# Moving the operand ring and the weights to multiples of 128 bytes, and splitting the first tile's gated layer by token blocks

## The chip, the core and the metric

The kernel runs on one NeuronCore of a Trainium2 chip. The metric is the device time of one execution in microseconds (us); lower is better. A NeuronCore has a matrix engine (PE, which also loads its stationary operands; those loads are shown as PEld), a vector engine (DVE), a scalar engine (ACT), a general engine (POOL) and a sync engine (SP). Each takes its own instructions in order, and semaphores order them against each other. Matmul operands lie in SBUF, an on-chip memory of 128 partitions, and results go to PSUM, which has 8 banks of 128 x 512 floats.

## The reference

The inputs are `x` (8 batches x 256 tokens x 256), `ctx` (8 x 120 x 256) and the ternary weights (-1, 0, 1) of a feed-forward net with a scale for each output feature.

```python
x = x + xattn(layernorm(x), ctx)        # per batch: gelu(xn ctx^T) * (xn ctx^T), times ctx
h = silu(lin(z, w1) * s1) * (lin(z, w2) * s2)   # z = layernorm(x); 256 -> 1024
h = gelu(lin(h, h1) * sh1)                      # 1024 -> 1024, exact gelu
h = gelu(lin(h, h2) * sh2)                      # 1024 -> 1024
x = x + lin(h, w3) * sw3                        # 1024 -> 256
```

Everything is float32.

## The kernel before

**Tiles and stages.** The 2048 tokens are four tiles of 512 tokens; a tile is two batches, a batch two token blocks of 128. The program runs in three stages that overlap only at their seams.

1. *Attention and gated layer* (`Attention.run`, lines 208 to 294, and `gated`, lines 418 to 454). For each batch: layernorm statistics on DVE (L232, L236, L237), the root on POOL (L242), the normalised rows `xn` (L252 on DVE, or L249 on ACT), PE transposes (L264), scores (L269), a tanh form of gelu on ACT and DVE (L282 to L287), values (L274), the residual (L290), a second layernorm, transposes again, and `finish` (L399, L400), which writes the transposed rows as two float32r tiles: `hi` is the rounded value and `lo` the rest, so that two passes of the faster float32r matmul give float32 accuracy. Then the gated layer: for each of 8 feature groups `m`, 8 matmuls (two sides, `hi` and `lo`, two halves of the contraction), a Silu on ACT (L450) and a product on DVE (L452).
2. *The two hidden layers* (`hidden`, lines 491 to 551), done on pairs of tiles by a seven-product scheme (Strassen-Winograd). `operand` (line 473) rounds an operand into a slot `hi` and the rest into `lo` (L480 on ACT, L484 on DVE); `product` (L511) runs, for each of four output groups, 4 matmuls of 128 x 512 on `hi` and 4 on `lo`. The slots are a ring of three pairs of tiles, `hi0..2` and `lo0..2`, made in `open_later` (line 611) in a pool on the right side of SBUF. The very first product uses another pair, `op0`, which lies on the left side beside the weights `w0..w6`. The stage has 864 matmuls on the ring and 32 on `op0`.
3. *The output layer* (`output`, L562): 256 matmuls of 128 x 256 with the ring's tiles as the stationary operand and `w3` as the moving one; then two DVE instructions (L297, L298) and a store (L582) for each token block.

**Order.** All of it is recorded in a `Plan`: every entry has an engine, a cost in us, what it reads and writes and a `lag` until its result can be used. `issue` (line 140) ranks the entries by the longest path behind them, changes some ranks by random seeds listed in `PICKS`, runs a list scheduler with these costs, and emits the instructions in the order that comes out. The costs of a matmul are `PE = 0.1185` for 256 columns and `PE2 = 0.2265` for 512 (lines 162, 163). Loads have a landing time, their `lag`: line 203 gives 2.2 us for the pieces of batch 0, 3.5 for batch 1 and 4.0 for all others; line 206 has 2.5 and 4.0 for the context.

**Names that the change touches.** `NORM_ON_ACT = 2` (line 43): from batch 2 on, the normalised rows come from ACT, with an extra DVE instruction (L239) and POOL instruction (L244) for it. `HALVED = 2` (line 42): tiles 0 and 1 run the gated layer by batches, so that its matmuls have 256 columns; tiles 2 and 3 by the whole tile, 512 columns. `turn` (line 414) hands out PSUM banks 0 to 4 in rotation. `const` and `keep` are pools on the left of SBUF, filled upwards; `early` and `later` are on the right, filled so that their end is fixed.

Of the kernel before, what the change touches and what calls it, by code (L numbers as in the profile page):

```python
# [10 lines left out]
F32 = mybir.dt.float32  # L11
# [9 lines left out]
P = 128  # L21
NB = 8
S = 256
# [8 lines left out]
RING = 3  # L32

PICKS = (
    17, 35, 50, 83, 119, 135, 167, 184, 208, 217, 248, 283, 296, 346, 414, 434, 469, 491, 533,
    575, 610, 675, 710, 726, 818, 898, 1040, 1072, 1715, 1745, 1774, 1894, 1946, 2086, 2179,
    2192, 2221, 2298, 2311, 2410, 2929, 3422, 4202, 4298, 4888, 5025, 5171, 5227, 5233, 5618,
    5767, 5867, 6269, 9944, 11293, 46856, 46885, 47139, 49461,
)
FORCE_GENERAL = False  # L40

HALVED = 2
NORM_ON_ACT = 2

# [18 lines left out]
class Plan:  # L65
# [6 lines left out]
    def add(self, engine, weight, emit, r=(), w=(), lag=0.2, early=0.0, chain=None):  # L72
        i, deps = len(self.ops), {}
        for k in r:
            if k in self.writer:
                deps[self.writer[k]] = True
            self.readers.setdefault(k, []).append(i)
        for k in w:
            if k in self.writer:
                deps[self.writer[k]] = True  # L80
            for j in self.readers.pop(k, ()):
                if j != i:
                    deps[j] = True
            self.writer[k] = i
        if chain is not None:
            if chain in self.last:
                deps.setdefault(self.last[chain], False)
            self.last[chain] = i
        self.ops.append((engine, weight, emit, deps, lag, early))
# [72 lines left out]
PE = 0.1185  # L162
PE2 = 0.2265
# [3 lines left out]
def xattn_ffn_kernel(ctx: ExitStack, tc: tile.TileContext, x, ctx_b, wall, scal, s3, out):  # L167
    nc = tc.nc
    const = ctx.enter_context(tc.tile_pool(name="const", bufs=1))
# [7 lines left out]
    s3b = const.tile([P, D], F32, name="s3b")  # L177
    bad = const.tile([P, 1024], BF16, name="bad")
    flag = const.tile([1, 1], I32, name="flag")

    class Attention:

# [11 lines left out]
        def load(self, plan, b, pieces):  # L194
            i = b % self.loads
            xv = x[b * S : (b + 1) * S, :].rearrange("(j p) d -> p j d", p=P)

            def load_x(js):
                nc.sync.dma_start(self.xb[i][:, js, :], xv[:, js, :])  # L199

            for js in pieces:
                plan.dma("SP", 0.45, lambda js=js: load_x(js), 0.128 * (js.stop - js.start),
                         lag=(2.2, 3.5)[b] if b < 2 else 4.0,
                         w=[("xb", i, j) for j in range(js.start, js.stop)])
            plan.dma("SP", 0.45, lambda: nc.sync.dma_start(self.cb[i], ctx_b[b]), 0.25,  # L205
                     lag=2.5 if b < 2 else 4.0, w=[("cb", i)])

        def run(self, plan, b, js, bank, bank_key, x1, x1_key, finish, early):

# [12 lines left out]
            ve, rs, nm, sh = (v[i][:, js] for v in (self.ve, self.rs, self.nm, self.sh))  # L222
            on_act = b >= NORM_ON_ACT
            halves = bank[:, : 2 * n].rearrange("p (k c) -> p k c", k=2)
# [76 lines left out]
    with ExitStack() as es, ExitStack() as wide:  # L301
# [13 lines left out]
        start = es.enter_context(ExitStack())  # L315
# [4 lines left out]
        w12 = early_pool.tile([P, 4, 1024], F32R, name="w12")  # L320
        xT = [[early_pool.tile([P, 2, N], F32R, name=f"xT{i}{j}") for i in range(2)] for j in range(2)]
# [4 lines left out]
        add = plan.add  # L326
# [13 lines left out]
        def load_layer(layer, order, gate=()):  # L340
            for name in order:
                plan.dma("POOL", 0.8, lambda name=name: nc.gpsimd.dma_start(
                    weight(layer, name).rearrange("p m k c -> p m (k c)"), block_rows(layer, name)),
                    1.05, r=gate, w=weight_keys(layer, name), chain="weights", lag=4.0)
# [64 lines left out]
                    w=[("x1s", 2 * b + j) for j in range(js.start, js.stop)], lag=4.0)  # L409


        turns = [0]

        def turn():
            turns[0] += 1
            return (turns[0] - 1) % 5

        def gated(t, c=None):


            cs = (0, 1) if c is None else (c,)
            n, cols = len(cs) * S, slice(cs[0] * S, (cs[-1] + 1) * S)

            def products(m, sides):
                for side in range(2):
                    for i in range(2):
                        for k in range(2):
                            first = i == 0 and k == 0
                            nc.tensor.matmul(  # L429
                                sides[side],  # L430
                                lhsT=w12[:, m // 2, (((m % 2) * 2 + side) * 2 + k) * P :][:, :P],
                                rhs=xT[t % 2][i][:, k, cols],
                                start=first and (c is None or side == 0),
                                stop=i == 1 and k == 1 and (c is None or side == 1),
                                skip_group_check=True)

            for m in range(8):
                if c is None:
                    banks = [turn(), turn()]
                    sides = [mm[i] for i in banks]  # L440
                else:
                    banks = [turn()] * 2
                    sides = [mm[banks[0]][:, i * n : (i + 1) * n] for i in range(2)]
                b0, b1 = sides
                i = 2 * t + m // 4
                o, okey = q[i][:, m % 4, cols], [("q", i, m % 4)]
                add("PE", 8 * (PE2 if c is None else PE), lambda m=m, sides=sides: products(m, sides),
                    r=[("w12", m // 2)] + [("xT", t % 2, c, j) for c in cs for j in range(2)],
                    w=[("mm", i) for i in set(banks)], chain="main", lag=0.3)
                add("ACT", act(n), lambda o=o, b0=b0, m=m: nc.scalar.activation(  # L450
                    o, b0, AF.Silu, scale=sc[:, m : m + 1]), r=[("mm", banks[0]), "sc", "table"], w=okey)
                add("DVE", dve(n) - 0.03, lambda o=o, b1=b1, m=m: nc.vector.scalar_tensor_tensor(  # L452
                    o, o, sc[:, 8 + m : 9 + m], b1, op0=ALU.mult, op1=ALU.mult),
                    r=[("mm", banks[1])], w=okey)
# [146 lines left out]
        for c in (0, 2):  # L601
            plan.dma("POOL", 0.8, lambda c=c: load_w12(c), 1.05, r=[("first", 0, 0)],
                     w=[("w12", c), ("w12", c + 1)], chain="weights")
# [7 lines left out]
        def open_later():  # L611
            wide.close()
            pool2 = open_pool(es, "later", side="right", reuse_waits="tile")
            later["hi"] = [pool2.tile([P, 4, N], F32R, name=f"hi{i}") for i in range(RING)]
            later["lo"] = [pool2.tile([P, 4, N], F32R, name=f"lo{i}") for i in range(RING)]
            later["w3"] = pool2.tile([P, 2, 1024], F32R, name="w3")
            later["o"] = [pool2.tile([P, D], F32, name=f"o{i}") for i in range(3)]
            later["x1"] = [pool2.tile([P, D], F32, name=f"x1_{i}") for i in range(6)]

        gated(0, 0)  # L620
        gated(0, 1)
        for t in range(1, NT):
            for b in (2 * t, 2 * t + 1):
                attention(b, both, (5 + (b + 1) % 3,), 6.0)
            for c in (0, 1) if t < HALVED else (None,):
                gated(t, c)
        load_layer(0, ("11", "12", "21", "22"), [("first", 4, 0)])
        sum_weights(0, (S1, S2, S4, S3))
        add("POOL", 0.0, open_later, w=[("xT", i, c, j) for i in range(2) for c in range(2) for j in range(2)] +
            [("w12", c) for c in range(4)] + [("xb", i, j) for i in range(4) for j in range(2)] + ["later"])  # L630
        plan.dma("POOL", 0.8, lambda: nc.gpsimd.dma_start(
# [39 lines left out]

    with tc.If(inexact == 0 if FORCE_GENERAL else inexact != 0):
        with ExitStack() as es:
# [8 lines left out]
            for c in range(NCH):  # L682
                w = wpool.tile([P, 1024], F32, tag=f"g{c}", name=f"g{c}")
# [3 lines left out]
            xT = gbuf.tile([P, 2, S], F32, name="xTg")  # L687
            x1 = gbuf.tile([P, 2, D], F32, name="x1g")
            bank = ppa.tile([P, N], F32, name="gpa")
            for b in range(NB):  # L690
# [33 lines left out]
                for j in range(2):  # L724
                    po = pout.tile([P, D], F32, tag="po", name="pog")
                    for k in range(8):
# [3 lines left out]
                            start=(k == 0), stop=(k == 7))  # L730
# [43 lines left out]
```

## Time and profile before

| | us |
|---|---|
| median of three executions | 343.33 |
| lowest and highest of them | 341.93, 345.07 |
| the profiled execution | 345.08 |
| its span, first to last instruction | 343.0 |

The profile shows one execution. In the rows by line, a line number is that of the kernel, `x` is a count, and `mm<-hi,w` reads: output tile `mm`, operands `hi` and `w`. A time in the first column is the start from the beginning of the span. Busy times of matmuls are those of single records, which overlap: what a matmul costs in a dense stream is the distance from its start to that of the next one, not its own duration. The three stages lie at about 0 to 96 us, 96 to 305 us and 305 to 336 us.

### The profile page before, as it was taken

To read this page: it belongs to the slowest core of one execution; us is meant where nothing else is said; L and a number is where in the kernel's file an instruction comes from. 1 tells how busy PE (TensorE), PEld (TensorE's weight loads), DVE (VectorE), ACT (ScalarE), POOL (GpSimd) and SP (SyncE) were. 2 spreads that over 40 slices of the span, in tenths; PEclk is the share of its full clock that TensorE was granted. 3 is DMA by queue.
4 is the path that set the end of the run, shared out by engine and by line. 5 is a ranking of instruction groups with operands and counts; after the bars stand their busy time and mean duration, and the time that the engine had idled before them with its cause. 6 is when DMAs were issued, how large, how long until landed. Compare 5 with 4: busy or idle time off the path is not lost.

```text
span 343.0 us, 4574 instructions
## 1 busy us (share of the span) xinstructions
PE 325.9 (95%) x1670; PEld 274.8 (80%) x1670; DVE 261.4 (76%) x432; ACT 215.2 (63%) x316; POOL 50.0 (15%) x69
## 2 busy tenths in 40 slices
PE   2599999999999999999999999999999999999992
PEld 1399999888888888888888888888888888889991
DVE  5768788999888747997457998947997655728972
ACT  2356777664489787666767765688677665656500
POOL 4216111220004141011111210031002000000000
PEclk9989999999999999999999999999999999999998
DMA  7946940163007279047928950038008000003442
GB/s 242 314 129 180 385 142 10 53 185 124 0 0 76 24 116 143 12 92 184 225 50 187 181 95 0 0 33 91 0 1 94 0 0 3 0 0 94 123 124 70
DMA packets 22381, 32.43 MB, mean 95 GB/s; under 512 B 1744, under 2 KB 15184, under 8 KB 22352
## 3 DMA queue, kind: packets, MB, share of 16 engines
q0 software_dynamic: 10256, 17.30, 27.5%
q1 hardware_dynamic: 12096, 14.77, 13.8%
q8 instruction: 15, 0.25, 0.3%
q14 instruction: 14, 0.11, 0.1%
HBM read 33.64 MB, written 4.19 MB: 110 GB/s over the span
## 4 chain that ended last, share of the span: by engine, by line
PE 93%; DVE 2%; DMA 2%; SPq 1%; issue 0%; DVEq 0%
PE mm L511 61%; PE mm L429 17%; PE mm L562 9%; PE mm L274 2%; DMA xb<-x_d 2%; PE mm L264 2%; PE mm L269 2%; DVE ln_st L232 1%; SPq L205 1%; SPq L199 0%; DVE xb L290 0%; DVE o L297 0%; DVE xn L252 0%; DVE ge L287 0%; DVE o L298 0%
## 5 line engine op out<-in xcount | busy, mean ns | idle before, releaser
L511 PE MATMUL mm<-hi,w 128*128 128x512 f32 x432 | 118.4, 395 | 0.0
L511 PE MATMUL mm<-lo,w 128*128 128x512 f32 x432 | 118.4, 395 | 0.0
L484 DVE TENSOR_TENSOR lo<-q,hi 128x1024 fp32r<-128x1024 f32 x70 | 83.8, 1220 | 21.3 <-ACT hi L480 21.3
L511 PEld LDWEIGHTS mm<-lo,w 128*128 128x128 f32 x432 | 81.0, 187 | 19.8
L511 PEld LDWEIGHTS mm<-hi,w 128*128 128x128 f32 x432 | 80.9, 187 | 19.8
L480 ACT CAST hi<-q 128x1024 fp32r<-128x1024 f32 x70 | 70.1, 1045 | 9.7 <-PE mm L562 7.9
L429 PE MATMUL mm<-xT,w 128*128 128x256 f32 (+1 forms) x384 | 65.2, 325 | 0.0
L429 PEld LDWEIGHTS mm<-xT,w 128*128 128x128 f32 x384 | 56.4, 191 | 5.3
L526 DVE TENSOR_TENSOR q<-q,mm 128x512 f32<-128x512 f32 x48 | 32.9, 687 | 26.8 <-PE mm L511 26.0
L530 ACT ACTIVATE q<-q,sc 128x512 f32<-128x512 f32 x48 | 34.4, 723 | 27.0 <-DVE q L526 27.0
L368 POOL DMA_DIRECT2D d<-wall_d x22 | 24.6, 1156 | 129.5 <-ACT d L366 129.5
L520 ACT COPY q<-mm 128x512 f32<-128x512 f32 x48 | 27.9, 587 | 24.1 <-PE mm L511 24.1
L450 ACT ACTIVATE q<-mm,sc 128x256 f32<-128x256 f32 (+1 forms) x48 | 26.1, 543 | 24.0 <-PE mm L429 23.7
L503 DVE TENSOR_TENSOR q<-q,q 128x1024 f32<-128x1024 f32 x32 | 38.1, 1219 | 0.0
L452 DVE SCALAR_TENSOR_TENSOR q<-q,sc,mm 128x256 f32<-128x256 f32 (+1 forms) x48 | 26.7, 565 | 7.0 <-ACT q L450 3.7
L350 DVE TENSOR_TENSOR w<-w,w 128x512 fp32r<-128x512 f32 x32 | 21.1, 687 | 5.6 <-DMA w<-wall_d 5.6
L366 ACT ACTIVATE d<-w 128x1024 bf16<-128x1024 f32 x22 | 23.0, 1055 | 0.0
L562 PE MATMUL mm<-w,hi 128*128 128x256 f32 x128 | 20.7, 284 | 0.0
L562 PE MATMUL mm<-w,lo 128*128 128x256 f32 x128 | 20.6, 283 | 0.0
L242 POOL TENSOR_TENSOR ln_rs<-ln_ve,eps_exp 128x2 f32<-128x2 f32 (+1 forms) x18 | 12.3, 682 | 49.2 <-DVE ln_nm L239 43.5
L264 PE MATMUL mm<-ident,xn 128*128 128x128 f32 x64 | 10.9, 300 | 8.0 <-DVE xn L252 8.0
L562 PEld LDWEIGHTS mm<-w,hi 128*128 128x128 f32 x128 | 17.7, 192 | 0.1
(50 smaller groups left out, 206.8 us busy)
## 6 DMA issues: line engine op xcount, KB each, us to landing
w<-wall_d POOLq DMA_DIRECT2D x11, 1024.0 KB, 8.2
d<-wall_d POOLq DMA_DIRECT2D x22, 256.0 KB, 6.0
w<-wall_d SPq DMA_DIRECT2D x8, 512.0 KB, 3.6
x<-x1s SPq DMA_DIRECT2D x16, 128.0 KB, 2.6
out_d<-o SPq DMA_DIRECT2D x16, 128.0 KB, 2.1
cb<-ctx_d SPq DMA_DIRECT2D x8, 248.0 KB, 3.9
xb<-x_d SPq DMA_DIRECT2D x7, 256.0 KB, 3.5
x1s<-xb SPq DMA_DIRECT2D x7, 256.0 KB, 2.4
```

Of the source, the lines that this page charges most:

```text
L368: plan.dma("POOL", 0.8, lambda: nc.gpsimd.dma_start(d4, src, accum_op=ALU.add), 1.04, w=[("d", i)], lag=8.0)
L429: nc.tensor.matmul(sides[side], lhsT=w12[:, m // 2, (((m % 2) * 2 + side) * 2 + k) * P :][:, :P], rhs=xT[t % 2][i][:, k, cols], start=firs ...
L450: add("ACT", act(n), lambda o=o, b0=b0, m=m: nc.scalar.activation(o, b0, AF.Silu, scale=sc[:, m : m + 1]), r=[("mm", banks[0]), "sc", "tab ...
L452: add("DVE", dve(n) - 0.03, lambda o=o, b1=b1, m=m: nc.vector.scalar_tensor_tensor(o, o, sc[:, 8 + m : 9 + m], b1, op0=ALU.mult, op1=ALU.m ...
L480: nc.scalar.copy(slot_views(i)[0][:, ms], q[src][:, ms])
L484: nc.vector.tensor_sub(l[:, ms], q[src][:, ms], h[:, ms].bitcast(F32))
L503: add("DVE", dve(1024), lambda ms=ms: nc.vector.tensor_tensor(q[into][:, ms], q[x][:, ms], q[y][:, ms], op=ALU.subtract), r=q_keys(x, ms) ...
L511: nc.tensor.matmul(mm[bank], lhsT=w[:, m, k, :], rhs=part[:, k, :], start=(p in OPENS and kind == 0 and k == 0), stop=(p in CLOSES and kin ...
L520: add("ACT", act(512), lambda: nc.scalar.copy(q[i][:, m], mm[bank]), r=[key], w=[("q", i, m)])
L526: add("DVE", dve(512), lambda: nc.vector.tensor_tensor(o(), o(), mm[bank], op=ALU.add), r=[key], w=[("q", i, m)])
L530: add("ACT", act(512, 1), lambda: nc.scalar.activation(o(), src(), AF.Gelu, scale=sc[:, col : col + 1]), r=["sc", "table"] + ([] if p in a ...
L562: nc.tensor.matmul(mm[banks[j]][:, :D], lhsT=part[:, k, j * P : (j + 1) * P], rhs=later["w3"][:, r, k * D : (k + 1) * D], start=(r == 0 an ...
```

## The change

Four things are edited.

- **Addresses.** A tile of 64 bytes per partition is added to `const` and one of 96 bytes to `later`. In the built program, with byte addresses within a partition:

| tile | before | mod 128 | after | mod 128 |
|---|---|---|---|---|
| `w0` (others follow by 8192) | 73664 | 64 | 73728 | 0 |
| `op0` `hi`, `lo` | 143296, 151488 | 64 | 143360, 151552 | 0 |
| `hi0` (the ring follows by 8192) | 162784 | 96 | 162688 | 0 |
| `w3` | 211936 | 96 | 211840 | 0 |
| `w12`, `xT` (gated layer) | 161344, 177728 | 64 | 161344, 177728 | 64 |

- **Gated layer of tile 0.** It ran in two halves of 256 tokens; it now runs block 0, block 1, then blocks 2 and 3 together, so that half of it has matmuls of 128 columns. The plan's cost for such a matmul is 0.066 us.
- **Norms.** `NORM_ON_ACT` goes from 2 to 4: batches 2 and 3 are normalised on DVE.
- **Landing times and order.** The plan reckons 7.0 us for the loads of batch 2, and 3.0 and 4.0 us for the context of batches 0 and 1. `PICKS` is another list, and the bank rotation starts at 3.

```diff
+ALIGN, ALIGN_RIGHT = 16, 24
+FIRST = (range(1), range(1, 2), range(2, 4))
-NORM_ON_ACT = 2
+NORM_ON_ACT = 4
...
     flag = const.tile([1, 1], I32, name="flag")
+    const.tile([P, ALIGN], F32, name="align")
...
-                         lag=(2.2, 3.5)[b] if b < 2 else 4.0,
+                         lag=(2.2, 3.5, 7.0)[b] if b < 3 else 4.0,
...
-                     lag=2.5 if b < 2 else 4.0, w=[("cb", i)])
+                     lag=(3.0, 4.0, 7.0)[b] if b < 3 else 4.0, w=[("cb", i)])
...
-        turns = [0]
+        turns = [3]
...
-        def gated(t, c=None):
-            cs = (0, 1) if c is None else (c,)
-            n, cols = len(cs) * S, slice(cs[0] * S, (cs[-1] + 1) * S)
+        def gated(t, js=range(4)):
+            n, cols = len(js) * P, slice(js[0] * P, (js[-1] + 1) * P)
+            wide_bank = len(js) == 4
...
-                add("PE", 8 * (PE2 if c is None else PE), lambda m=m, sides=sides: products(m, sides),
-                    r=[("w12", m // 2)] + [("xT", t % 2, c, j) for c in cs for j in range(2)],
+                add("PE", 8 * {1: 0.066, 2: PE, 4: PE2}[len(js)], lambda m=m, sides=sides: products(m, sides),
+                    r=[("w12", m // 2)] + [("xT", t % 2, j // 2, j % 2) for j in js],
...
+            pool2.tile([P, ALIGN_RIGHT], F32, name="align_right")
-        gated(0, 0)
-        gated(0, 1)
+        for js in FIRST:
+            gated(0, js)
...
-            for c in (0, 1) if t < HALVED else (None,):
-                gated(t, c)
+            for js in (range(2), range(2, 4)) if t < HALVED else (range(4),):
+                gated(t, js)
```

**The queues after.** The order of products in the hidden and output layers stays as it was. At the start, SP's first seven loads were x block 0, x block 1, x of batch 1, the contexts of batches 0, 1 and 3, the scales; x of batch 3 and the context of batch 2 followed, and x of batch 2 came last. They are now x block 0, x of batch 1, x block 1, x of batch 2, the contexts of batches 0 and 1, x of batch 3. On POOL the first of the two `w12` loads now stands between the roots of block 0 and block 1, where both stood behind both roots. On PE the first gated matmul stood behind the second-norm transposes of both blocks of batch 0, the values of batch 1 and the first transposes of batch 2; now it stands behind the second-norm transposes of block 0 and the values of batch 1. Gated groups follow fp32 matmuls of the attention 19 times where it was 17.

## The prediction

> **What bounds the kernel.** I read the page's shares first, then the chain that ended last, in order of time, then the starts of PE's matmuls.
>
> ```profile
> PE 325.9 (95%) x1670; PEld 274.8 (80%) x1670; DVE 261.4 (76%) x432; ACT 215.2 (63%) x316; POOL 50.0 (15%) x69
> ...
> PE   2599999999999999999999999999999999999992
> ...
> PE 93%; DVE 2%; DMA 2%; SPq 1%; issue 0%; DVEq 0%
> ```
>
> PE is busy in every slice but the first two and the last, and 93% of the chain is PE. So whatever lengthens or shortens PE's stream between 20 and 336 us is paid in full; work of other engines there is hidden. The pieces of the chain that carry the rest:
>
> ```profile
> 5.04 6.57 DMA xb<-x_d
> ...
> 11.63 0.75 DVE ln_st L232 x2
> ...
> 27.42 5.75 PE mm L429 x48
> ...
> 76.33 19.99 PE mm L429 x88
> 96.32 208.86 PE mm L511 x896
> 305.18 28.79 PE mm L562 x240
> ```
>
> A start, a length, a count: 5.75/48 = 119.8 ns per gated matmul of 256 columns, 19.99/88 = 227.2 at 512 columns, 28.79/240 = 120.0 in the output layer, but 208.86/896 = 233.1 in the hidden layers, also 512 columns. PE's timeline at the seam tells why:
>
> ```profile
> 96.15 7.42 PE L511 MATMUL mm<-op,w 128*128 128x512 f32 x32
> 103.41 1.10 PE L511 MATMUL mm<-hi,w 128*128 128x512 f32 x4
> 104.35 1.10 PE L511 MATMUL mm<-lo,w 128*128 128x512 f32 x4
> 105.28 1.10 PE L511 MATMUL mm<-hi,w 128*128 128x512 f32 x4
> ```
>
> From start to start, `op0` takes (103.41 - 96.15)/32 = 226.9 ns; the ring, same line, shape and weights, (105.28 - 103.41)/8 = 233.8 (single steps over the stage average 233.4). `op0` and `w` lie at 64 mod 128, the ring at 96. An address seems to cost 6.5 ns a matmul.
>
> The second thing to see is how long a stationary operand takes to load when nothing covers it. Just after the flag's tiny matmul PE's queue is empty, and line L562 shows, between 334.0 and 334.2 us (durations least, median, most; starts):
>
> ```profile
> L562 PEld LDWEIGHTS mm<-w,hi x2: 186/188/189, 334.0 to 334.1; 128*128 128x128 f32 x2
> L562 PE MATMUL mm<-w,hi x1: 386/386/386, 334.0 to 334.0; 128*128 128x256 f32 x1
> ```
>
> This first matmul is recorded with 386 ns, where the line's median is 283: it waited 103 ns for its own load, and the second load started when it could begin. In the dense stream each load starts 2 to 3 ns after the preceding matmul, so one load is ahead, not two.
>
> **The skill.** *TensorE: Matmul & The Clock Gate*, "LDWEIGHTS (loading the stationary operand)", gives columns/1.2 in ns, 107 for 128; the 103 above agrees. Its "Back-to-back issue gap" gives 512/2.4 + 2.5, about 216 ns, for a matmul alone; no float32r row here gets there (226.9 is the best). *SBUF — State Buffer*, "Operand start alignment", speaks of legality and says that its runs timed nothing, so no page prices the alignment. *DMA: Bandwidth & Descriptors* has a fixed cost near 2 us; block 0's load (issue 0.74, landing 2.8) agrees.
>
> **The change part by part** (us; the sum is made against the profiled execution, 345.08).
>
> 1. *Ring at 0 mod 128.* 864 matmuls by 233.4 - 226.9 = 6.5 ns: **-5.6**. No row has a matmul at 0 mod 128. Bounds: nothing gained (0), or down to the skill's 216 (864 x 17.4 = -15.0, with 256 output matmuls from 120 to 109 another -2.8). I take `op0`'s value. `op0`, `w12`, `xT` and the output layer, where both operands had the same place mod 128 already, stay as they are. DVE (75% busy in 106 to 200) and ACT (73%) have room for a PE that is 3% faster.
>
> 2. *Half of tile 0 in 128-column matmuls.* 64 matmuls of 256 columns (64 x 119.8 = 7.7) become 128. The plan reckons 66 ns each, which would be 8.5, +0.9. But each still needs its own load of 128 columns, which starts with the matmul before it: the 103 to 107 ns, not the 53 ns of streaming, set the pace. I take 109, the step of the loads in the idle case: 128 x 109 = 14.0, **+6.3**. Bounds: +0.9 and, at the 120 of today's stream, +7.7. ACT and DVE get 8 more Silus and 8 more products of 128 columns for the same data; a `gq` of 120x128 takes 0.29, so a group needs some 0.3 on each against 0.87 on PE: hidden, and with PE as slow as today they would wait at most the 0.5 a planned group lasts.
>
> 3. *Start.* Today DVE sits from 10.29 to 11.63 before L232 of batch 2, whose load was issued last (5.04) and took 6.57; `ge` of block 1 and the residual stand behind it. Afterwards this load is SP's fourth: 768 KB are ahead of or in it, and today 512 KB had landed at 5.1 and 760 at 5.8, so it is there by about 6.3 and the stall goes. What is late next: x of batch 1 goes ahead of block 1 on SP, so block 1 comes at about 4.9 instead of 3.3, and DVE's L232 for it stands *before* block 0's norm: norm at 5.85 against 4.73, and the first transposes with it. Walking the queues on from there with today's durations: scores of block 0 at 7.4 (context landed by 6.8), transposes of batch 1 at 10.5, values of block 0 at 11.2, batch 1's scores until 13.3, its `gq` at 13.8 with block 0's second statistics queued behind, norm of block 0 at 15.7, values of batch 1 from 16.9 to 18.9 (2.07, as today at the low clock), the gated layer at **18.9**. Today it starts at 19.46, but with six more transposes done (6 x 109 = 0.65). Net **+0.1**; bounds -1.5 (landings earlier than read) and +1.5. Ahead of POOL's second root stands one `w12` issue (0.8), done long before that root can start; the weights land at 14.6 and 17.3 today, ahead of need.
>
> 4. *Smaller.* Two more changes from fp32 matmuls into the gated stream, about 0.08 each: +0.2. The first three gated matmuls cost 0.4 extra at the low clock today (360, 213, 210 ns); load-bound ones lose less: -0.3. PE's one stall inside the stream, at 64.25 to 65.20, where values of a batch wait for DVE's `ge` (0.84, and 0.1 of load): with PE some 6 us behind its plan, DVE and ACT are ahead and it goes: **-0.9**; bounds -0.9 and +1.
>
> 5. *Norms of batches 2 and 3 on DVE.* Eight L252 at 0.41 against eight L249 at 0.59 on ACT; four L239 (0.185) and four L244 on POOL go. DVE gets 3.3 - 0.7 = 2.6 more up to 40 us, where it is busy 8.2 and 7.0 of 10; the stretched PE stream covers it: 0. Without that cover (66 ns matmuls) some 1 of it would show.
>
> 6. *Landing times, seeds, bank rotation* act through the order alone, counted in 3 and 4. The end is untouched: the last products, L297, L298 and stores come in the same order, 0.
>
> Sum: -5.6 + 6.3 + 0.1 + 0.2 - 0.3 - 0.9 = -0.2. The profiled execution becomes 344.9; it lies 1.75 above the median, so the median becomes about **343.1**.
>
> **Rivals.**
>
> *A. The 128-column matmuls run at the plan's 66 ns* (loads run further ahead than the records show). Against: the idle case, and the start of each load. For: the record of a load may be modelled. Then item 2 is +0.9 and DVE's cover is thinner: with +1.0 for it and the stall staying, 343.3 - 5.6 + 0.9 + 0.1 - 0.1 + 1.0 = 339.6; with neither, 337.7. I take **339**.
>
> *B. 0 mod 128 is better than 64.* For: every fast row still lies 11 ns above the skill's gap, and 64 may be half a cure. Against: 227 at 512 and 120 at 256 columns differ by just 256/2.4, so the 11 to 13 ns look like a fixed cost of the load. If half of it goes, 864 x 5.5 + 1.4 = -6.2: **337**; if all, 331.
>
> *C. The cost lies in the distance of the operands, not in the address* (slower). All fast rows have operands a multiple of 512 bytes apart (`op0` to `w0` 69632, `xT` to `w12` 16384, `w3` to `hi0` 49152); the ring is 89120 away, 32 mod 512, and 88960 after, 384 mod 512. If 512 is what matters, the ring keeps 233 ns and the rest of the sum stands: 343.3 + 5.4 = **348.7**. It decides once a ring matmul still takes over 231.
>
> *D. The new order loses at the start*: block 1 later still, or DVE at its limit from 20 to 40 us, 3 to 5 us: **347**.
>
> **How the numbers follow.** About 1% (3.4 us) can be told from no change. Likeliest, load-bound and aligned: 0.50, range 340.5 to 346. A 0.17, B 0.13, C 0.11, D 0.09. The range of 8 in 10 takes in most of A and the nearer parts of B, C and D: 335.5 to 347.5. Faster: A 0.13, B 0.13, likeliest 0.05, together 0.31. Slower: C 0.10, D 0.07, likeliest 0.03, together 0.20. Within 1%: 0.49.
>
> **What would show it.** Ring matmuls 226 to 228 ns apart in the chain's piece of L511, about 203 long (right: 1; 233: C; below 222: B). The 128-column rows of L432 107 to 120 ns apart (67: A), and the hidden layers starting near 101 to 102 instead of 96. First gated matmul near 18.9. No DVE wait for `xb` near 11, one of 1 to 2 near 3.5. No PE gap near 65. The prediction is wrong if the hidden layers start at 96 or before, or if that piece is not about 5.6 shorter.

## The result and the profile after

| | before | after |
|---|---|---|
| median of four executions, us | 343.6 | 363.25 |
| lowest and highest | 341.93, 345.07 | 357.38, 368.61 |
| ratio, with its 95% interval | | 1.041 (1.035 to 1.047) |
| the profiled execution | 345.08 | 368.29 |
| its span | 343.0 | 366.5 |

The kernel became slower by 4%, outside the range of the prediction. Its executions lie further apart than those of the kernel before, and the ratio compares those near 358 alone, without the slower two at 368, with the kernel before. The trace read here is that of the first, at 368.29: what it shows of the clock is larger than what the executions near 358 can have lost to it. The two at 368 list a mean granted clock of 0.943, those near 358 one of 0.974 to 0.997. No trace of these was kept, and the listed mean can miss a low stretch at the start, as experiment 3 shows, so how long their clock was low stays open.

The page of the kernel after, the same rows as before and the clock's row beneath them (PEclk: granted clock of PE in tenths, one digit for each of 40 slices of 9.2 us):

```profile
PE 350.5 (96%) x1734; PEld 298.3 (81%) x1734; DVE 265.2 (72%) x444; ACT 214.9 (59%) x316; POOL 49.3 (13%) x65
...
PE   2699999999999999999999999999999999999993
...
PEclk9955559999999999999999999999999999999997
...
PE 94%; DMA 1%; ACT 1%; DVE 1%; SPq 0%; issue 0%
```

PE is still the bound and still busy everywhere, with 25 us more of it. The clock's row has what is new: four slices at half clock, from 18 to 55 us, in which PE is nonetheless fully busy. Its chain of waits, in order of time (start, length, what):

```profile
2.63 5.20 DMA cb<-ctx_d
...
16.15 0.97 DVE xn L255 x3
...
17.83 2.07 PE mm L277 x4
19.91 5.01 PE mm L432 x24
...
26.22 5.01 PE mm L432 x24
...
59.40 2.87 PE mm L432 x24
...
102.61 18.17 PE mm L432 x80
120.78 208.86 PE mm L514 x896
329.63 27.82 PE mm L565 x232
...
357.57 3.08 PE mm L565 x24
```

L432 is the gated layer (L429 before), L514 the hidden layers (L511), L565 the output (L562). Two readings carry the result of this execution. The hidden layers take 208.86 us for 896 matmuls, to the digit what they took before: aligning the ring gained nothing. And they begin at 120.78 instead of 96.32. The first three groups of 128-column matmuls take 5.01 us for 24 where 2.6 was predicted; 24 matmuls of twice the width, at 59.40, take 2.87. The seam to the ring, from PE's timeline:

```profile
120.61 7.43 PE L514 MATMUL mm<-op,w 128*128 128x512 f32 x32
127.88 1.09 PE L514 MATMUL mm<-hi,w 128*128 128x512 f32 x4
128.80 1.10 PE L514 MATMUL mm<-lo,w 128*128 128x512 f32 x4
129.74 0.63 PE L514 MATMUL mm<-hi,w 128*128 128x512 f32 x2
```

`op0` steps at (127.88 - 120.61)/32 = 227.2 ns, the aligned ring at (129.74 - 127.88)/8 = 232.5. Over the stage the ring's mean is 233.3, but its single steps changed: 229 and 237 to 238 ns by turns, where they were 231 to 235. The address does something; it is not this that makes it fast.

Busy times by stretch show the low clock (the fields: stretch, its length, then each engine's busy us and instructions, the mean clock, the DMA share and GB/s). Before:

```profile
20.00:40.00 20.00, 20.00 (x157) 19.49 (x156) 15.19 (x47) 15.34 (x33) 6.38 (x11) 0.99 0.80 237
```

After:

```profile
20.00:40.00 20.00, 20.00 (x93) 19.60 (x93) 7.04 (x24) 5.54 (x14) 1.43 (x2) 0.50 0.17 53
```

PE is busy for 20.00 of 20 us both times, and does 93 matmuls, most of them half as wide, instead of 157. ACT and DVE fall to less than half their work: they wait for PE. PE's busy share tells nothing of its clock.

### The profile page after: what moved, and what is told of

Its sections match the earlier page's. It is cut to its first block, busy times and chain, and to the rows that moved or that the text cites. A ratio compares the mean times of both kernels' runs of the same rounds, so it can differ in the third digit from the quotient of the medians.

```text
span 366.5 us, 4710 instructions
## 1 busy us (share of the span) xinstructions
PE 350.5 (96%) x1734; PEld 298.3 (81%) x1734; DVE 265.2 (72%) x444; ACT 214.9 (59%) x316; POOL 49.3 (13%) x65
## 4 chain that ended last, share of the span: by engine, by line
PE 94%; DMA 1%; ACT 1%; DVE 1%; SPq 0%; issue 0%
PE mm L514 57%; PE mm L432 21%; PE mm L565 8%; PE mm L272 3%; PE mm L277 2%; PE mm L267 2%; DMA cb<-ctx_d 1%; SPq L202 0%; ACT xn L252 0%; DVE xn L255 0%; ACT q L453 0%; ACT xT L402 0%; DVE o L300 0%; DVE o L301 0%; DVE gq L286 0%
## 5 line engine op out<-in xcount | busy, mean ns | idle before, releaser
L514 PE MATMUL mm<-lo,w 128*128 128x512 f32 x432 | 118.5, 395 | 0.0
L514 PE MATMUL mm<-hi,w 128*128 128x512 f32 x432 | 118.4, 395 | 0.0
L514 PEld LDWEIGHTS mm<-lo,w 128*128 128x128 f32 x432 | 81.2, 188 | 19.6
L514 PEld LDWEIGHTS mm<-hi,w 128*128 128x128 f32 x432 | 81.1, 188 | 19.6
L487 DVE TENSOR_TENSOR lo<-q,hi 128x1024 fp32r<-128x1024 f32 x70 | 83.6, 1219 | 14.1 <-ACT hi L483 14.1
L432 PE MATMUL mm<-xT,w 128*128 128x256 f32 (+2 forms) x448 | 86.5, 361 | 0.0
L432 PEld LDWEIGHTS mm<-xT,w 128*128 128x128 f32 x448 | 77.1, 235 | 6.0 <-DVE xT L403 0.4
L453 ACT ACTIVATE q<-mm,sc 128x256 f32<-128x256 f32 (+2 forms) x56 | 28.1, 504 | 43.2 <-PE mm L432 42.8
L455 DVE SCALAR_TENSOR_TENSOR q<-q,sc,mm 128x256 f32<-128x256 f32 (+2 forms) x56 | 28.1, 515 | 21.3 <-ACT q L453 19.9
L565 PE MATMUL mm<-w,hi 128*128 128x256 f32 x128 | 20.7, 284 | 0.0
L565 PE MATMUL mm<-w,lo 128*128 128x256 f32 x128 | 20.6, 283 | 0.0
L267 PE MATMUL mm<-ident,xn 128*128 128x128 f32 x64 | 12.9, 329 | 7.8 <-DVE xn L255 7.7
L565 PEld LDWEIGHTS mm<-w,hi 128*128 128x128 f32 x128 | 17.7, 192 | 0.1
```

The lines of the kernel that those rows point to most:

```text
L432: nc.tensor.matmul(sides[side], lhsT=w12[:, m // 2, (((m % 2) * 2 + side) * 2 + k) * P :][:, :P], rhs=xT[t % 2][i][:, k, cols], start=firs ...
L487: nc.vector.tensor_sub(l[:, ms], q[src][:, ms], h[:, ms].bitcast(F32))
L514: nc.tensor.matmul(mm[bank], lhsT=w[:, m, k, :], rhs=part[:, k, :], start=(p in OPENS and kind == 0 and k == 0), stop=(p in CLOSES and kin ...
L565: nc.tensor.matmul(mm[banks[j]][:, :D], lhsT=part[:, k, j * P : (j + 1) * P], rhs=later["w3"][:, r, k * D : (k + 1) * D], start=(r == 0 an ...
```

## The experiments

Two questions were open: why the ring did not speed up (the address, or rival C's distance between the two operands), and why the stage before the hidden layers took some 24 us more in the trace where 6 were reckoned (narrow matmuls as such, the clock, or the new order). The ratios below are taken against executions of the kernel before that were measured along with each run; their medians are 344.05 to 344.33.

**1. The narrow matmuls alone.** The kernel before, its order untouched; each matmul of tile 0's first half is issued as two of 128 columns.

```diff
+SPLIT = (0, 0)
...
+            pieces = 2 if (t, c) == SPLIT else 1
...
-                            nc.tensor.matmul(
-                                sides[side],
+                            for h in range(pieces):
+                                w = n // pieces
+                                nc.tensor.matmul(
+                                    sides[side][:, h * w : (h + 1) * w],
...
-                                rhs=xT[t % 2][i][:, k, cols],
+                                    rhs=xT[t % 2][i][:, k, cols][:, h * w : (h + 1) * w],
...
```

> The kernel before, with the same order of instructions on every engine, in which each 256-column matmul of the gated layer's first half of tile 0 is issued as two of 128 columns. Theory 1 (the loads of the stationary operand set the pace and nothing else): these rows 107 to 120 ns apart, +6 us, 349 to 350 us, clock as before. Theory 2 (a load-bound stream also keeps PE's clock at half): rows 213 ns apart, the low clock lasts 15 to 40 us more in the trace, 128 x 213 = 27 us where 7.7 stood, together with slower attention matmuls +15 to +25 us, 358 to 368 us, and different from execution to execution. Rival (the new order at the start is what costs): 344 to 345, no change.

Measured 351.03 against 344.2, ratio 1.019 (1.012 to 1.027). PE's timeline:

```profile
17.94 3.66 PE L434 MATMUL mm<-xT,w 128*128 128x128 f32 x16
21.39 2.00 PE L270 MATMUL mm<-xnT,cb 128*120 128x256 f32 x4
22.83 6.07 PE L434 MATMUL mm<-xT,w 128*128 128x128 f32 x48
```

Sixteen matmuls take 3.66 us at half clock, 213 ns from start to start; in the 48 that follow, the clock comes back at 23.7, and from there the step is 110 to 115 ns, mean 111.7. So a load-bound step of 112 ns is real: 128 x 111.7 = 14.3 us for 7.7, +6.6, which is item 2 of the prediction within 0.3. The half clock lasts 6.8 us here and 3.4 in the kernel before: at most half of the difference, 1.7, is lost by it (an estimate). Narrow matmuls alone explain some 7 us, neither the 24 of the trace above nor the 14 of the executions near 358; the 15 to 25 that the second theory forecast did not come.

**2. The change without narrow matmuls.** `FIRST = (range(2), range(2, 4))` in the kernel after: tile 0 in halves again, everything else as changed.

> The changed kernel with the gated layer of tile 0 in two halves of 256 tokens again; the addresses, the landing times, the norms on DVE and the seeds stay changed. Theory 2: the clock rises near 20 us as before and all of the loss goes, 340 to 346 us. Theory 1: 350 to 352 (only 6 of the loss of 14 goes). Rival (order, norms, landing times cost): 352 or more, with PE gaps at the start.

Measured 350.26, ratio 1.020 (1.013 to 1.026). With wide matmuls the clock stays full from 10.9 to 65.5 us. But another list of work makes another order, since the seeds act on an entry's position in that list. Its chain:

```profile
62.37 0.39 ACT ge L285
62.76 0.02 issue
62.79 0.42 DVE gq L286
63.21 0.60 DVE xb L293
63.81 1.13 DVE op L487
64.94 0.34 DVE ge L290
...
98.06 207.14 PE mm L514 x888
...
312.75 1.78 DVE lo L487 x2
```

PE waits near 63 us behind an operand's rest (`op`, L487) that DVE does ahead of `ge`, and again near 313, now in the output stage, for `lo`. So its total, which falls into the range of the first theory but not for its reason, says little about the change. Two things stand: without narrow matmuls the hidden layers begin at 98.06, not 120.78, and 888 ring and `op0` matmuls in 207.14 us are 233.3 ns each: the addresses bring nothing in this order either.

**3. Both paddings alone**, in the kernel before: ring and weights at 0 mod 128, the order untouched.

```diff
+    const.tile([P, 16], F32, name="align")
...
+            pool2.tile([P, 24], F32, name="align_right")
```

> The kernel before with only the two paddings of the change: ring, weights and w3 at 0 mod 128, the order untouched. If the trace of the changed kernel reads rightly (229 and 237 ns in turn, mean 233.3), no gain: 343 to 344 us. If the alignment works and the changed kernel's slow ring came from something else: 337 to 338.

Measured 344.59, ratio 1.001 (0.999 to 1.004) over 20 executions. The chain:

```profile
20.34 1.56 PE mm L430 x8
...
26.08 0.96 PE mm L430 x8
...
97.23 208.86 PE mm L512 x896
```

The two paddings bring nothing by themselves. The trace has a second lesson. Its first eight gated matmuls take 1.56 us, eight later ones 0.96: until 21.6 us their steps are 213 ns, those of half clock. Yet the clock's row of its page shows no low slice (8.6 us each):

```profile
PEclk9999999999999999999999999999999999999997
```

So the row, and the mean that an execution lists, can show full clock over a low stretch at the start; the distance of the starts is the safer witness.

**4. The distance.** One padding of 32 bytes instead: the ring goes to 162752, which is 64 mod 128 like the weights, and 89088 = 174 x 512 from `w0`.

```diff
+            pool2.tile([P, 8], F32, name="align_right")
```

> The kernel before with the ring moved down by 32 bytes, so that ring and weights are a multiple of 512 bytes apart (both at 64 mod 128). Distance theory (rival C of the prediction): ring matmuls 227 ns apart, the piece of L511 203 us long, total 337.5 to 338.5. If an address at 0 or 64 mod 128 decides nothing and the distance neither (the ring is slow because it alternates between two tiles): 233 ns, 343 to 344.

Measured **338.12** against 344.2, ratio 0.983 (0.977 to 0.989), faster than both kernels. The chain:

```profile
96.56 203.10 PE mm L511 x896
299.65 28.79 PE mm L562 x240
```

203.10/896 = 226.7 ns: the whole 5.7 us.

**5 and 6. Address or distance?** `both96` moves the weights by 32 bytes and leaves the ring, so that both lie at 96 mod 128 (padding of 8 floats on the left). `ring256` moves the ring by 288 bytes (72 floats on the right), so that the distance is 173.5 x 512.

> The kernel before with the weights, op0 and what lies behind them on the left moved by 32 bytes, the ring left where it is: ring at 96 mod 128 as before, weights now at 96 too, distance 89088 = 174 x 512. Theory (distance of the two operands, a multiple of 512): ring matmuls 226.7 ns apart, time near 338. Rival (the absolute place counts, and 96 is worse than 64): 233 ns, time 344, and op0's 32 matmuls slow down as well to 233.

> The kernel before with the ring moved by 288 bytes: ring and weights both at 64 mod 128 and 64 mod 256, distance 88832 = 173.5 x 512. If operands must lie a whole multiple of 512 apart: ring matmuls 233 ns apart, time 344. Rival (equal place within 128 or 256 bytes is enough): 226.7 ns, time 338.

338.92, ratio 0.984 (0.979 to 0.990), and 339.53, ratio 0.988 (0.985 to 0.991). The chain of `both96`:

```profile
95.95 203.13 PE mm L512 x896
```

and of `ring256`:

```profile
95.50 203.10 PE mm L511 x896
```

Neither an address of 96 mod 128 nor a half multiple of 512 costs anything. What the fast cases share so far is the distance, 0 mod 256: rival C had the right cause, but a whole multiple of 512 is not needed.

**7, 8 and 9. Other distances**: paddings of 56, 24 and 4 floats on the right, nothing else.

> The kernel before with the ring moved by 224 bytes: it lies at 162560, 0 mod 128, and 88896 from the weights, 64 mod 256. Theory (only a distance of 0 mod 256 is fast): ring matmuls 233 ns apart on average, time near 344. Rival (a multiple of 64 is enough where the ring alone moves): 227 ns, 338.

> The kernel before with the ring moved by 96 bytes, the weights left: the ring lies at 162688, 0 mod 128, where the kernel after has it, but 89024 from the weights, 192 mod 256. Same theory: 233 ns, near 344. Rival (the ring's own multiple of 128 helps once the weights are not moved with it): 227 ns, 338.

> The kernel before with the ring moved by 16 bytes: 80 mod 128, and 89104 from the weights, 16 mod 256. Theory (any distance other than 0 mod 256 costs, an overlap of the two reads that starts over every 256 bytes): 229 to 234 ns, near 342 to 344. Rival (a distance below 32 bytes is as good as none): 227 ns, 338.

One execution each: 339.85, 342.06 and 338.47. The chain of `ring_d64`:

```profile
95.42 205.04 PE mm L511 x896
```

of `ring_d192`:

```profile
93.94 208.86 PE mm L511 x896
```

and of `ring_d16`:

```profile
96.29 203.10 PE mm L511 x896
```

The steps of the ring, over all the kernels:

| distance ring to weights, mod 256 | step of a ring matmul, ns | kernels |
|---|---|---|
| 0 | 226.7 | moved by 32 or 288; both at 96; `after_both`, `ring512_warm` below |
| 16 | 226.7 | moved by 16 |
| 32 | 233.3 (231 to 235) | before |
| 64 | 228.9 (225 to 232) | moved by 224 |
| 128 | 233.3 (229 and 237) | after; both paddings; `after_halves`, `after_warm` |
| 192 | 233.3 | moved by 96 |

For 64 and for 16 the expectation from the theory was wrong: 64 costs a third of the full price, 16 nothing. With the ring at 0 mod 128, the address that the change gives it, `ring_d192` is slow and `ring_d64` nearly fast; the ring's own address doesn't decide. Nor does that of the weights: with them at 64 mod 128 the ring was slow in the kernel before and in `ring_d192`, fast in `ring512`, `ring256` and `ring_d16`. Only 0 was measured at both 0 and 256 mod 512, so for the other rows the period of 256 is not shown, and no run shows the mechanism behind the table.

**10. The clock.** The kernel after, with 16 matmuls of 128x512 zeros in bfloat16 into a bank that is free then, 7 before the first transposes and 9 in the wait before the gated layer. They are work added, for the clock only; the order of the plan's entries stays.

```diff
+            def transposes(first=[True]):
+                if first[0] and b == 0 and js.start == 0 and warm:
+                    first[0] = False
+                    warm["go"](7)
...
+                if b == 0 and js.start == 1 and warm:
+                    warm["go"](9)
...
+        def go(n):
+            for _ in range(n):
+                nc.tensor.matmul(mm[4], lhsT=bad[:, :P], rhs=bad[:, :N], start=True, stop=True)
```

> The kernel after, with 16 extra matmuls of 128x512 zeros in bfloat16 into a PSUM bank that is free then: 7 ahead of the first transposes, 9 behind the values of batch 1, block 1, so that PE is not idle just before the gated layer. Theory (the dense stream of load-bound 128-column matmuls cannot bring the clock back up once it has fallen, so the clock must be high when it begins): the gated layer starts at full clock, its 128-column rows are 108 to 115 ns apart instead of 213, the hidden layers start near 102 to 106 instead of 120.8, and the time is 350 to 354. Rival (the stream itself pulls the clock down, or the low clock of the profile is not what separates 363 from 350): rows of 213 ns come back within the stream, time 357 to 368.

Measured **349.67**, just under the range expected, lowest and highest 349.55 and 349.92, ratio 1.016 (1.013 to 1.019). From its page:

```profile
PEclk9999999999999999999999999999999999999999
```

and its chain:

```profile
17.83 0.87 PE mm L282 x4
18.70 2.73 PE mm L445 x24
...
25.64 2.63 PE mm L445 x24
...
102.77 208.86 PE mm L527 x896
```

Groups of 24 narrow matmuls (L445 here) fall from 5.01 to 2.63 us, the values before them from 2.07 to 0.87, and the hidden layers begin 18 us sooner. The first slices of the row are not to be trusted here either: of the nine added matmuls ahead of the gated layer, the two that start before 15.9 last 627 and 634 ns each, the later ones mostly 379. From there on the steps bear the row out. The median is 7.7 to 8.5 us below the executions of the kernel after near 358, and some 18.7 below the two at 368. In the traces, what the added matmuls change is the clock. If the clock is also what the executions near 358 lost, they spent some 15 to 17 us at half of it (an estimate: twice 7.7 to 8.5); no trace of them shows it.

Narrow matmuls that begin at full clock keep it here and in `after_both`; begun at half clock, they stayed there for 37.5 us in the profiled execution of the kernel after and for 6.8 in `split_first`. In the six traces with matmuls of 256 columns in this place whose records hold such a low stretch (the kernel before, `ring512`, `both96`, `ring256`, `ring_d64`, `ring_d16`), it lasts 3.4 us each time.

**11. Both faults taken away.** The same kernel with the ring 128 bytes further down (0 mod 128, distance 0 mod 256): `ALIGN, ALIGN_RIGHT = 16, 56`.

> The kernel after with both faults taken away: the ring moved by another 128 bytes (both operands at 0 mod 128, distance 88832, 0 mod 256) and the 16 extra matmuls that keep the clock up. If the two act alone and add, the time is that of the kernel after with the extra matmuls, 349.7, less 864 x 6.6 ns = 5.7: 344, level with the kernel before, the 128-column rows having taken what the ring gives. Rival (they overlap: a faster PE now waits for DVE and ACT at 65 to 70 us and in the hidden layers): 346 or more.

Measured 344.02, ratio 0.998 (0.997 to 1.000) over 20 executions. Its chain:

```profile
18.88 2.63 PE mm L445 x24
...
102.84 203.11 PE mm L527 x896
305.94 27.83 PE mm L578 x232
...
333.89 3.07 PE mm L578 x24
```

The two add: 349.67 - 5.7 = 344.0. Everything that the change does beyond these two, the narrow matmuls above all, costs what the ring can give, and the kernel is back where it was.

**12. The best version.** The kernel before with the ring moved by 32 bytes and the 16 matmuls of zeros.

> The kernel before with the ring moved by 32 bytes (a multiple of 512 from the weights) and the same 16 extra matmuls. If the low clock at the start of the gated layer costs what the records of before show there (values at half clock 2.07 for 0.87, the first gated rows 213 for 120 over some 3 us), the time falls by 1.5 to 3 below the 338.1 of the moved ring alone: 335 to 336.6. Rival: what ends last at the start is DVE and the loads, not PE, and the extra matmuls stand in the way: 338 or more.

Measured **336.74**, ratio 0.978 (0.975 to 0.980), just above the range expected and the fastest of all. Its chain:

```profile
18.48 0.95 PE mm L442 x8
...
94.77 203.10 PE mm L524 x896
```

Its first eight gated matmuls take 0.95 us, at full clock, and the hidden layers begin 1.8 us sooner than in `ring512`. The intervals of the two ratios overlap, though, and `ring_d192` shows full clock at this place, and a start at 93.94, with no matmul added. So the 5.7 us of the distance are shown; 1 to 2 us from the added matmuls are likely, no more.

## Why the prediction was wrong

**Item 1 failed (-5.6; measured 0).** The measurement behind it was right: `op0` 226.9, ring 233.4, 6.5 ns a matmul, 5.7 us to be had. The step that failed is "An address seems to cost 6.5 ns": of two properties that set `op0` apart, its address and its distance to the weights, I took the first, though no row had a matmul at 0 mod 128 and the list of fast rows under rival C spoke for the second in every entry. Rival C held: the ring keeps 233 ns. It got a chance of 0.11, and its 348.7 is near the 349.67 of `after_warm`, the same kernel with the clock up before its gated layer; what is left up to the measured time belongs to item 4 below.

**Item 2 held at full clock (+6.3; measured +6.6)**, by `split_first` and `after_warm`: 112 ns a matmul, as reckoned from the load, not the plan's 66. Rival A fell. (64 x 119.8 against 128 x 66 makes +0.8 for the plan, not the +0.9 written there; nothing hangs on it.) The Trainium skill's price for a load, 107 ns (*TensorE: Matmul & The Clock Gate*, "LDWEIGHTS (loading the stationary operand)"), lies 5 ns below the measured step at full clock.

**Item 4's line on the clock failed (-0.3; measured +17 in the profiled execution, some 8 in those near 358 if the clock is all that they lost).** "The first three gated matmuls cost 0.4 extra at the low clock today; load-bound ones lose less." They lose the same factor of two: 213 ns for 112. And I took for granted, without a reason, that the low clock ends after 3.4 us as today. Between the first gated matmul and the first of `op0` the profiled execution of the kernel after spends 101.27 us, `after_both` 84.15; of these 17.1 us, 13.4 are in the 128-column matmuls, 1.0 in the 256-column ones, 2.7 in the attention's between them. The Trainium skill, *TensorE: Matmul & The Clock Gate*, "Part 1: The HAM clock gate", says that the clock halves after an idle window of about 3.4 us and doubles after a busy one. The durations agree (3.41 us in the kernel before, 6.8 in `split_first`, 37.5 after: one, two and eleven times as long), but here PE was busy throughout, by its records, and the clock stayed down for eleven windows. A possible reason, not shown: if a 256-column matmul streams for all of its 213 ns at half clock, one of 128 columns, which takes 213 ns too, streams for half of them (an estimate), so that the array would rest for the other half although PE's record reads busy.

**The stall near 65 went**, as item 4 said: in `after_both` and in the kernel after, PE's records run on without a gap there. The rest of item 4 was too small. Between the same two marks `after_both` takes 7.45 us more than before: 6.05 in the gated matmuls of tiles 0 and 1, 0.5 in the transposes (six more of them, 0.65, less the stall's 0.8 would have made -0.2), 0.5 in scores and values, 0.4 in the 512-column matmuls. I had 0.2 for switching between kinds; about 1.6 came, spread over many places.

**Item 3 (+0.1) was nearly right for time, in part by luck.** The first gated matmul stands at 19.35 (predicted 18.9, before 19.46). DVE's wait near 11 is gone. But the first norm comes at 5.13, where I had 5.85, and the context of batch 0 lands at 7.83, where I had 6.8, and becomes the piece of the chain that ends last there; the first scores begin at 7.97, not 7.4.

**Item 5 (0) was nearly right**: two of the norms that the change moved to DVE stand there at 16.07 and 16.39, ahead of block 0's second norm, whose root was done at 16.53 and which starts at 16.71; the three are the 0.97 of `xn` on the chain. That is some 0.2 us (an estimate from these times), and `after_both` has the same three on its chain. **Item 6 missed a gain of 0.9 at the end**: the flag's matmuls (L664 before, L668 after) now stand ahead of 24 output matmuls, not 16, so that, it seems, less of DVE's work is left behind the last of PE's. From the end of PE's last matmul to the end of the span it is 6.8 us before, 5.9 after.

The account of the profiled executions closes so: the hidden layers begin 24.5 later (7.45 + 17.1 between the marks, 0.1 less at the start), the ring takes the same, the end is 0.9 shorter: 23.5, the difference of the spans. For the executions near 358, some 14 above before, the 17.1 would be about 8.

## What to carry to other kernels

When two rows differ, list every property in which they differ, and test the cheapest edit for each alone: one padding of 32 bytes would have told address from distance before anything else was built on it. Narrowing a matmul below the time of its load costs the load's time; and where such matmuls begin at half clock, the clock may stay there. PE's busy share doesn't show that: look at the clock's row first, and at the distance of the starts, since the row can miss a low stretch at the beginning. And costs that are predicted at full clock hold only if the clock is full where the work is moved.

## What the runs showed of the hardware

- A float32r matmul of 128x512 with a stationary load each takes 226.7 ns or up to 233.4 (6.6 more), by the distance in SBUF between its two operands, here given modulo 256 bytes: 0 and 16 fast, 64 at 228.9, 32, 128 and 192 slow. Fast rings lay at 0, 64, 80 and 96 mod 128, slow ones at 0 and 96.
- A float32r matmul of 128 columns with its own load takes 112 ns at full clock and 213 at half, so it gains nothing over 256 columns (120 and 213).
- PE's clock stayed at half for 37.5 us while such matmuls and those of the attention followed one another without a gap; the same stream begun at full clock kept it.
- The record of the granted clock can show full over a low stretch at the start: 1.0 in `pads_only` until 21.6 us, with steps of 213 ns where 120 are those of full clock.
